# Scheduling priorities by place in an image's course, for a four-stage kernel on pairs of images

## The chip, the cores and the metric

The kernel runs on one core of a Trainium2 chip. The metric is the device time of one execution in microseconds (us). Engines are named PE (TensorE, matrix products), PEld (its weight loads), DVE (VectorE), ACT (ScalarE), POOL (GpSimd) and SP (SyncE, which here only issues transfers). DMA means the core's 16 transfer engines. A line such as L1442 is line 1442 of the kernel before; the change inserts lines, so in the kernel after the same statement stands up to 24 lines lower. This text always uses the numbers of the kernel before, except where it shows a profile of the kernel after.

## What is computed

The input is 16 images of 56x56 positions with 128 channels, in float32. Each image goes through four layers, one after the other. Each adds its result to a running image (the last writes the sum out) after a group norm with 32 groups:

```
x = x + window_attention(gn(x))   # 7x7 windows, shifted by 3; 4 heads; softmax; output product
x = x + triangle(gn(x))           # layer norm, gated products, product over k, layer norm, gate
x = x + fourier(gn(x))            # 2D Fourier modes: attention over the 56 rows as tokens, then two
                                  # operators on modes with a GELU between, instance norms
x = x + bilinear(gn(x))           # products with SiLU, 3x7 convolutions, per-position 16x16 products
```

No layer mixes images, so images are independent. Within an image almost everything depends on what stands before it.

## The kernel before

The kernel is one long program without loops at run time. `tile_blocks` goes over the images b = 0 to 15 and for each writes out load, window attention, triangle, Fourier, bilinear. Images alternate between two **lanes** (`lane[0] = b % 2`). Each lane has its own large work buffer (the arena, one per lane), its own small buffers and its own PSUM banks; the running images `xt` share a pool of two. So two images can be in work at once, and image b+2 can begin only when image b has given up its lane's arena and its `xt`.

The order of the instructions on each engine isn't written by hand. A scheduler takes the program, keeps a model of each engine's time, and whenever an engine is free gives it, of the instructions whose inputs and buffers are ready, the one with the best (lowest) priority number. The priority is a counter of the context, `tc.cur_priority`, that rises as the program is traced. So in the kernel before, every instruction of image b comes ahead of every instruction of image b+1, where both are ready; image b+1 fills what is left. The result is a fixed order for each engine, which then runs it strictly in that order; semaphores make it wait where needed. DMA issues stand in the queue of the engine that issues them: SP the loads, stores and most of bilinear's transfers, ACT bilinear's writes to DRAM, POOL the table's.

The parts of one image that the steps of the prediction name:

- **Load** (L450 to L457): seven transfers, transposes on PE, a copy on ACT. Then the group norm of each layer (L420 to L440), a chain of small steps.
- **Window attention** (L527 to L625): eight rows of windows, each a chain of products, softmax and products.
- **Triangle** (L628 to L735): the two layer norms, the gated products in two parts (L689 to L715), a turn (L724), the gate.
- **Fourier, first part** (L1155 to L1175): column modes (L918), scores (L1104) on DVE, and the modes called x3 (L1174).
- **Fourier, table loop** (L1203 to L1235): 8 steps of 8. Each step fetches 2 x 294 KB of a table from DRAM on POOL's queue (L1209), multiplies on DVE (L1211) and contracts on PE. There are eight slots for what is fetched.
- **Fourier, tail** (L1238 to L1301): a first inverse transform, then two operators (`operator`, L918 to L1032), each a chain of modes, product, inverse and norm; Gelu (L1290) ends the first.
- **Bilinear** (L1330 to L1510): 7 steps, each with project (SiLU, L1354), convolutions, and contractions. A contraction writes one tile eight times over to DRAM (L1342, 1.8 MB, ACT's queue), reads it back spread over partitions (L1439, 448 KB each, SP's queue), multiplies on DVE (L1442) and sums on PE (L369, L372).

The lines around the change are these:

```
    for b in range(NB):
        lane[0] = b % 2
        xt = load_image(b)
        done = False
        for s in stages:
            done = run[s](b, xt)
```

Of the kernel before, what the change touches and what calls it, by code (L numbers as in the profile page):

```python
# [54 lines left out]
ROWC = NW * WIN  # L55
NEG = -1.0e30
SN = math.sqrt(28.0 * 64.0)


def _rho(r, cut):  # L60
# [248 lines left out]
def tile_blocks(ctx: ExitStack, tc: tile.TileContext, ins, out, at, stages=(0, 1, 2, 3)):  # L309
# [17 lines left out]
    ps2 = [pool(f"ps2_{k}", 1, space=PSUM) for k in range(2)]  # L327

    lane = [0]
    count = [0]  # L330

    def uid(s):
# [127 lines left out]
    def store_image(b, xt):  # L460
        for q in range(NCH):
# [8 lines left out]
                in_=t[:TT, :].rearrange("p (a c) -> p a c", a=4),  # L470
            )

    env = dict(locals())
    blocks = [_window_attention, _triangle, _fourier, _bilinear]
    run = {s: blocks[s](env) for s in stages}
    for b in range(NB):
        lane[0] = b % 2
        xt = load_image(b)
        done = False
        for s in stages:  # L480
            done = run[s](b, xt)
        if not done:
            store_image(b, xt)
# [7 lines left out]
def _window_attention(env):  # L491
    e = _Env(env)
# [34 lines left out]
    def run(b, xt):  # L527
# [8 lines left out]
        for k in range(2):  # L536
            nc.gpsimd.memset(ar[:, k * half_arena + ROWC : k * half_arena + 408], 0.0)
        for wi in range(NW):
            o = wi % 2 * half_arena
            xw, qt, vt, st, atn, ot = (  # L540
                ar[:, o + a : o + a + n]
# [84 lines left out]
def _triangle(env):  # L626
    e = _Env(env)
    nc, mm, tt, ts, act, C, W, bc = e.nc, e.mm, e.tt, e.ts, e.act, e.C, e.W, e.bc  # L628
    eps = e.persistent("eps1", [P, 1], 1e-5)
    HC = 32  # L630

    def layer_norm(chunk, dst, sqs, lw, lb):


        for q in range(NCH):
            d, sq = dst[:, q * CH : (q + 1) * CH], sqs[:, q * CH : (q + 1) * CH]
            src = chunk(q)
            p = e.psb()
            mm(p[:, :CH], lhsT=C("cen"), rhs=src, start=True, stop=True)
            act(sq, p[:, :CH], AF.Square)  # L640
            nc.vector.tensor_copy(d, p[:, :CH])

        pv = e.psb()
        e.together(
            dict(
                out=pv[32 * (q % 4) : 32 * (q % 4) + 32, :CH],
                lhsT=C("oh")[:, 1 - q // 4 : 33 - q // 4],
                rhs=sqs[:, q * CH : (q + 1) * CH],
                start=q < 4,
                stop=q > 2,  # L650
            )
            for q in range(NCH)
        )
        rs = e.w2()
        act(rs[:, :CH], pv[:, :CH], AF.Sqrt, bias=eps)
        nc.vector.reciprocal(rs[:, :CH], rs[:, :CH])
        for q in range(NCH):
            d = dst[:, q * CH : (q + 1) * CH]
            p = e.psb()
            row = 32 * (q % 4) + q // 4  # L660
            mm(p[:, :CH], lhsT=C("ident")[:, row : row + 1].to_broadcast([P, P]), rhs=rs[:, :CH], start=True, stop=True)
            tt(d, d, p[:, :CH], ALU.mult)
            act(d, d, AF.Identity, bias=W("ln")[:, lb : lb + 1], scale=W("ln")[:, lw : lw + 1])

    def run(b, xt):
        nm, rs = e.group_norm(xt)
        ar = e.arena()
        xh = ar[:, 0:3144]
        nc.gpsimd.memset(xh[:, NTOK:], 0.0)

        def normed(q):
            t = e.w2()
            ts(t[:, :CH], xt[:, q * CH : (q + 1) * CH], nm, rs, ALU.add, ALU.mult)
            return t[:, :CH]

        sqs = ar[:, 10312 : 10312 + NTOK]
        layer_norm(normed, xh, sqs, 0, 1)

        l3, r3 = (ar[:, o : o + T * HC].rearrange("p (c i) -> p i c", i=T) for o in (3144, 4936))
        o3 = ar[:, 6728 : 6728 + 64 * T].rearrange("p (j c) -> p c j", c=64)
        for part in range(2):
            for g in range(T // 8):
                p = e.psd()
                for i in range(8):
                    c0 = (8 * g + i) * T
                    for half, w in ((0, "w1a"), (64, "w1b")):
                        mm(  # L689
                            p[half : half + 64, i // 4, i % 4 * P : (i % 4 + 1) * P],  # L690
                            lhsT=xh[:, c0 : c0 + 64],
                            rhs=W(w).rearrange("p (k c) -> p k c", c=64)[:, :, HC * part : HC * part + HC],
                            start=True,
                            stop=True,
                        )
                pv = p.rearrange("p a (i c) -> p (a i) c", c=P)
                sg = e.w2()
                s3 = sg.rearrange("p (i c) -> p i c", c=64)
                act(s3, pv[:, :, 64:128], AF.Sigmoid)
                tt(l3[:, 8 * g : 8 * g + 8, :], pv[:, :, 0:32], s3[:, :, 0:32], ALU.mult)  # L700
                nc.vector.scalar_tensor_tensor(  # L701
                    r3[:, 8 * g : 8 * g + 8, :], pv[:, :, 32:64], 1.0 / T, s3[:, :, 32:64], ALU.mult, ALU.mult
                )
            for g in range(4):
                for half in (0, 64):
                    p = e.psb()
                    s = slice(half, half + T)
                    for c in range(8):
                        mm(p[s, c * T : (c + 1) * T], lhsT=l3[s, :, 8 * g + c], rhs=r3[s, :, 8 * g + c], start=True, stop=True)
                    dst = o3[s, 8 * (4 * part + g) : 8 * (4 * part + g + 1), :]  # L710
                    src = p[s, :CH].rearrange("p (c j) -> p c j", j=T)
                    if half:
                        nc.scalar.copy(dst, src)
                    else:
                        nc.vector.tensor_copy(dst, src)  # L715

        on = ar[:, 3144 : 3144 + NTOK]
        on3 = on.rearrange("p (i j) -> p j i", j=T)
        for g in range(T // 8):
            p = e.psb()  # L720
            for j in range(8):
                for half in (0, 64):
                    s = slice(half, half + T)
                    mm(p[half : half + 64, j * T : (j + 1) * T], lhsT=o3[s, :, 8 * g + j], rhs=C("ident")[s, half : half + T], start=True, stop=True)  # L724
            nc.scalar.copy(on3[:, 8 * g : 8 * g + 8, :], p[:, :CH].rearrange("p (j i) -> p j i", i=T))
        layer_norm(lambda q: on[:, q * CH : (q + 1) * CH], on, sqs, 2, 3)
        for q in range(NCH):
            s = slice(q * CH, (q + 1) * CH)
            pg, py = e.psb(), e.psb()
            mm(pg[:, :CH], lhsT=W("gout"), rhs=xh[:, s], start=True, stop=True)  # L730
            mm(py[:, :CH], lhsT=W("pout"), rhs=on[:, s], start=True, stop=True)
            sg = e.w2()
            act(sg[:, :CH], pg[:, :CH], AF.Sigmoid)
            tt(sg[:, :CH], py[:, :CH], sg[:, :CH], ALU.mult)
            tt(xt[:, s], xt[:, s], sg[:, :CH], ALU.add)  # L735

    return run


def _fourier(env):  # L740
    e = _Env(env)
# [145 lines left out]
    def inorm(y, k):  # L887

        _, rs = centered(y)
        ts(rs, rs, sc[:, k : k + 1], None, ALU.mult)  # L890
        scaled(y, y, rs, k)
# [144 lines left out]
    def attention(uv, ar):  # L1036
# [3 lines left out]
        for s in range(2):  # L1040
# [4 lines left out]
            t = e.w2()  # L1045
# [7 lines left out]
        t = e.w2()  # L1053
# [20 lines left out]
        for name in ("dx", "dya", "dyb"):  # L1074
# [6 lines left out]
            else:  # L1081
                t = e.w2()
# [9 lines left out]

        n = 0
        for bank in range(2):
            sp = e.psb()
            for l0 in (0, 4):
                for c in range(2):
# [41 lines left out]
        for g in range(2):  # L1139
            p = e.psb()  # L1140
            for i in range(4):
                q = 4 * g + i
# [7 lines left out]
            ts(by_row(dst)[:, s], by_row(xt)[:, s], nm, rs, ALU.add, ALU.mult)  # L1150

    def run(b, xt):
        nm, rs = e.group_norm(xt)
        ar = e.arena()
        xa = ar[:, 7056:10640]  # L1155
# [10 lines left out]
        at = attention(uv, ar)  # L1166


        x3 = ar[:TT, : 3 * NM].rearrange("p (k n) -> p k n", k=3)
        for g in range(8):  # L1170
            p = e.psb()
# [23 lines left out]
        spec = x3[:, 0, :]  # L1195
        n = 0
        for q in range(8):
            s = slice(q * STEP, (q + 1) * STEP)
            if q % 2:
                pa, pb = e.psb(), e.psb()  # L1200
# [4 lines left out]
            for two in range(8):  # L1205
                t = slots[n % 8]
# [28 lines left out]
            nc.scalar.copy(spec[:, s], p)  # L1235


        y = ar[:, NM : NM + NTOK]  # L1238
        y3 = y.rearrange("p (t j) -> p j t", j=T)
        turned = ar[:, 7168 : 7168 + NTOK]  # L1240
# [30 lines left out]
        def residual(t0, p):  # L1271
            d = y[:, t0 * T : (t0 + 8) * T]
            tt(d, p, d, ALU.add)

        vs = ar[:, 5376 : 5376 + 4 * CH]
        inverse(ar, [spec], residual, vs)
        an = ar[:, 5376:8960]
# [4 lines left out]
        p12 = ar[:, 8960:12544]  # L1282
        f = ar[:, 0:3584]
        vs = ar[:, 3584:5376]
        operator(ar, an, "mw0r", "mw0i", f, p12, f, vs, 3)
        nc.gpsimd.memset(by_row(f, True), 0.0)
        for q in range(NCH):
            an8, f8 = (by_row(t)[:, 8 * q : 8 * q + 8] for t in (an, f))
            stt(f8, an8, sc[:, 12:13], f8, ALU.mult, ALU.add)
            act(f8, f8, AF.Gelu, bias=shift)  # L1290
        m = an
        operator(ar, f, "mw1r", "mw1i", m, p12, m, vs, 4, sc[:, 14:15])
        for q in range(NCH):
            m8, f8 = (by_row(t)[:, 8 * q : 8 * q + 8] for t in (m, f))
            stt(m8, f8, sc[:, 14:15], m8, ALU.mult, ALU.add)
        inorm(m, 5)
        for q in range(NCH):
            x8, m8 = (by_row(t)[:, 8 * q : 8 * q + 8] for t in (xt, m))
# [5 lines left out]
def _bilinear(env):  # L1304
    e = _Env(env)
# [9 lines left out]
    part = 96 * PLANE // P // 3  # L1315
# [7 lines left out]
        return bass.AP(tensor=t.tensor, offset=t.offset + start, ap=[list(d) for d in dims])  # L1323

    def run(b, xt):
        nm, rs = e.group_norm(xt)
        ar = e.arena()
        kv_dram = padded[e.lane[0]]
# [153 lines left out]
        queries, kern, feat = {q: project(q) for q in range(2)}, {}, {}  # L1482
        spread(0, 0)
        for q in range(NCH + 4):
            if 0 <= q - 4:
                last(q - 4, *feat.pop(q - 4))
            if q + 2 < NCH:
# [39 lines left out]
```

## Time and profile before

| what | value |
|---|---|
| median of 3 runs | 12942.06 us (12939.57 to 12974.12) |
| the profiled execution's own time | 12942.02 us |
| its span, first to last instruction | 12940.2 us |
| mean granted PE clock | 0.872 |
| DMA | 2092.81 MB, mean 162 GB/s |
| queues, share of 16 engines' span | SP's 19.1%, POOL's 17.7%, ACT's 13.3% |
| DVE L1442 | 2648.4 us in 1344, 2019 ns each |
| DVE L1211 | 1563.3 us in 1024, 1552 ns each |
| ACT table loads | 119 of 1283 ns |

How to read it: busy time is the union of an engine's instructions, and a share is of the span. The span can be cut into 40 equal slices, where a digit is the busy share in tenths; or into stretches of one's own choice, with the busy time of each engine and the DMA share in each. Idle time of an engine is put down to what came last before it went on, so of a wait for several things only the last is named. Matmul ends are modelled, so a busy PE isn't PE at its peak. A span is 1.9 us shorter than the execution's time, because what lies before the first and after the last instruction isn't in it.

### The profile page before, as it was taken

The page shows a single profiled execution, that of the slowest core. Times are in us where ns is not written, and L with a number is a line of the kernel's source. Part 1 is how long each engine was busy: PE and PEld are TensorE (multiplying, and loading weights), DVE is VectorE, ACT ScalarE, POOL GpSimd, SP SyncE. Part 2 cuts the span into 40 slices and gives each one's busy share as a digit, 9 for nine tenths or more (in the row PEclk, how much of TensorE's full clock was granted, in tenths as well). Part 3 has the DMA queues.
Part 4 walks back from the last instruction along what each step waited for, and adds up shares of the span by engine and source line. Part 5 has one row for each costly group of instructions (what it writes and reads, how often), then busy time and mean ns, then how long its engine had stood idle before and what let it go on. Part 6 is the DMA issues. An engine that isn't in the chain of part 4 may idle for free. (4 is left out here: it accounts for less than half of the span.)

```text
span 12940.2 us, 198571 instructions
## 1 busy us (share of the span) xinstructions
PE 9941.9 (77%) x81312; PEld 5481.7 (42%) x81312; DVE 9365.3 (72%) x12257; ACT 3739.1 (29%) x6439; POOL 2346.8 (18%) x3131
## 2 busy tenths in 40 slices
PE   7787678876888767887788876878768887687876
PEld 4443254442544325443254432544325453254532
DVE  7775777757777577775877757777577775867757
ACT  4322142231422314223142231422314223142321
POOL 0133001330012300123101230012300123001230
PEclk9887888888988889888898888988889888898888
DMA  1255902659026590355903569035690356903469
GB/s 36 58 182 195 341 29 69 171 199 334 32 83 157 198 339 28 87 153 203 342 21 82 158 210 338 18 92 148 212 333 21 96 145 234 324 8 106 134 236 317
DMA packets 1090458, 2092.81 MB, mean 162 GB/s; under 512 B 97936, under 2 KB 973712, under 8 KB 1089296
## 3 DMA queue, kind: packets, MB, share of 16 engines
q1 hardware_dynamic: 560000, 823.91, 19.1%
q0 software_dynamic: 163840, 616.76, 17.7%
q10 hardware_dynamic: 365712, 639.44, 13.3%
q8 instruction: 644, 10.55, 0.3%
q14 instruction: 262, 2.15, 0.1%
HBM read 1412.69 MB, written 667.03 MB: 161 GB/s over the span
## 5 line engine op out<-in xcount | busy, mean ns | idle before, releaser
L1442 DVE TENSOR_TENSOR arena<-arena 128x1792 f32<-128x1792 f32 x1344 | 2648.4, 2019 | 652.5 <-PE psb L372 349.3
L1211 DVE TENSOR_TENSOR arena<-arena 112x1344 f32<-112x1344 f32 x1024 | 1563.3, 1552 | 322.4 <-DMA arena<-table 310.4
L372 PE MATMUL psb<-arena,cst 128*32 128x448 f32 x9792 | 1505.2, 649 | 0.0
L1209 POOL DMA_DIRECT2D arena<-table x2048 | 1050.7, 515 | 2206.3 <-DMA arena<-table 496.5
L369 PE MATMUL psb<-arena,cst 128*32 128x448 f32 x1408 | 792.3, 650 | 813.7 <-DVE arena L1442 760.4
L372 PE MATMUL psb<-arena 128*64 128x448 f32 (+2 forms) x4864 | 1248.5, 534 | 0.0
L369 PE MATMUL psb<-arena 112*64 112x448 f32 (+1 forms) x1280 | 689.0, 624 | 374.2 <-DVE arena L1104 201.9
L417 POOL TENSOR_TENSOR arena<-arena,power 112x32 f32<-112x32 f32 x224 | 828.6, 3718 | 119.8 <-DVE arena L1373 118.4
L372 PE MATMUL psd<-arena 112*64 112x224 f32 (+1 forms) x3072 | 725.6, 457 | 0.0
L372 PEld LDWEIGHTS psb<-arena 112*64 112x64 f32 (+1 forms) x4864 | 455.3, 155 | 526.8 <-issue 521.1
L1427 ACT COPY arena<-psd 128x896 f32<-128x896 f32 x336 | 304.1, 906 | 1236.1 <-DVE arena L1442 656.6
L369 PE MATMUL psd<-arena 112*64 112x448 f32 x1024 | 539.9, 612 | 133.3 <-DVE arena L1211 117.6
L369 PEld LDWEIGHTS psb<-arena,cst 128*32 128x32 f32 x1408 | 120.3, 118 | 1211.5 <-DVE arena L1442 966.4
L1104 DVE TENSOR_TENSOR arena<-w,coef 128x1792 f32<-128x1792 f32 x256 | 508.0, 2018 | 81.4 <-PE psb L372 71.0
L372 PEld LDWEIGHTS psb<-arena,cst 128*32 128x32 f32 x9792 | 360.6, 123 | 448.2 <-issue 427.4
L372 PE MATMUL psd<-arena,wgt 128*32 128x448 f32 x2688 | 502.8, 608 | 38.8 <-DMA arena<-padded 38.3
L689 PE MATMUL psd<-wgt,arena 128*64 128x128 f32 x7168 | 493.3, 283 | 49.3 <-DVE arena L701 38.9
L369 PE MATMUL psd<-arena,wgt 128*32 128x448 f32 x896 | 440.7, 611 | 79.9 <-DMA arena<-padded 42.2
L689 PEld LDWEIGHTS psd<-wgt,arena 128*64 128x64 f32 x7168 | 425.4, 139 | 179.5 <-issue 126.8
L918 PE MATMUL psb<-cst,arena 128*128 128x64 f32 (+1 forms) x2688 | 447.6, 340 | 54.3 <-ACT arena L928 25.6
L918 PEld LDWEIGHTS psb<-cst,arena 128*128 128x128 f32 x2688 | 439.0, 255 | 93.2 <-issue 50.6
L1341 ACT COPY w<-psb 128x448 f32<-128x448 f32 x336 | 178.7, 532 | 1006.5 <-PE psb L372 749.9
(305 smaller groups left out, 18845.8 us busy)
## 6 DMA issues: line engine op xcount, KB each, us to landing
arena<-table POOLq DMA_DIRECT2D x2048, 294.0 KB, 9.1
dy<-w ACTq DMA_DIRECT2D x336, 1792.0 KB
arena<-dy SPq DMA_DIRECT2D x1344, 448.0 KB
arena<-padded SPq DMA_DIRECT2D x896, 162.8 KB
w<-x SPq DMA_DIRECT2D x112, 224.0 KB
out<-w SPq DMA_DIRECT2D x112, 224.0 KB
padded<-w ACTq DMA_DIRECT2D x336, 62.0 KB
padded<-arena SPq DMA_DIRECT2D x6, 449.5 KB
```

What stands on the lines that cost most here:

```text
L369: done = mm(**first)
L372: mm(**kw)
L417: ptt(dst, src, w, ALU.pow)
L689: mm(p[half : half + 64, i // 4, i % 4 * P : (i % 4 + 1) * P], lhsT=xh[:, c0 : c0 + 64], rhs=W(w).rearrange("p (k c) -> p k c", c=64)[:, : ...
L918: mm(p[:, 2 * i * nl : 2 * (i + 1) * nl], lhsT=src[:, t * P : (t + 1) * P], rhs=fc, start=True, stop=True)
L1104: tt(t4, bc(ys[c][:, l0 : l0 + 4, :], 1, 8), bc(coef[:, c, h0 : h0 + 8, l0 : l0 + 4], 3, T), ALU.mult,)
L1209: nc.gpsimd.dma_start(out=t[hh * T : (hh + 1) * T, :], in_=bc(tflat[q, two, hh], 0, T))
L1211: tt(t4, bc(x3[:, :, s], 1, 2), t4, ALU.mult)
L1341: nc.scalar.copy(t[:, :CH], p[:, :CH])
L1427: nc.scalar.copy(z, p[:, :, :CH])
L1442: tt(t4, bc(rep, 2, 2), bc(z, 1, 2), ALU.mult)
```

## The change

Each section of an image's course now sets the priority counter, instead of letting it run on from the start of the program. `at_time(t)` sets it to 100 times a place on a common axis: the origin of the image plus t. Origins of pairs are 1640 apart, and within a pair the odd image's origin is 100 later, a sixteenth. So an instruction of image 9 at place t of its course has the same priority as one of image 8 at place t + 100. The places follow the stages: windows 20 to 195, triangle 225 to 440, Fourier 475 to 1085 (x3 620, table loop 646 to 779, tail 800 to 1085), bilinear 1120 to 1550. The scheduler, its model of the engines and all instructions stay.

```diff
+BEAT, LEAD, COURSE, LAG = 100, 1000, 1640, 100
...
+    origin = [0]
...
+    def at_time(t):
+
+        tc.cur_priority = int(BEAT * (origin[0] + t))
+
     env = dict(locals())
     blocks = [_window_attention, _triangle, _fourier, _bilinear]
     run = {s: blocks[s](env) for s in stages}
     for b in range(NB):
         lane[0] = b % 2
+        origin[0] = LEAD + b // 2 * COURSE + b % 2 * LAG
+        at_time(0)
         xt = load_image(b)
...
         for wi in range(NW):
+            e.at_time(20 + 25 * wi)
...
     def run(b, xt):
+        e.at_time(225)
...
         for part in range(2):
+            e.at_time(300 + 40 * part)
...
+        e.at_time(380)
...
         layer_norm(lambda q: on[:, q * CH : (q + 1) * CH], on, sqs, 2, 3)
+        e.at_time(440)
...
     def run(b, xt):
+        e.at_time(475)
...
         for bank in range(2):
+            e.at_time(540 + 35 * bank)
...
+        e.at_time(620)
         x3 = ar[:TT, : 3 * NM].rearrange("p (k n) -> p k n", k=3)
...
         for q in range(8):
+            e.at_time(646 + 19 * q)
...
+        e.at_time(800)
         y = ar[:, NM : NM + NTOK]
...
+        e.at_time(858)
         vs = ar[:, 5376 : 5376 + 4 * CH]
         inverse(ar, [spec], residual, vs)
...
+        e.at_time(910)
         operator(ar, an, "mw0r", "mw0i", f, p12, f, vs, 3)
...
+        e.at_time(1000)
         operator(ar, f, "mw1r", "mw1i", m, p12, m, vs, 4, sc[:, 14:15])
...
+        e.at_time(1085)
         inorm(m, 5)
...
     def run(b, xt):
+        e.at_time(1120)
...
         for q in range(NCH + 4):
+            e.at_time(1170 + 38 * q)
```

## The prediction

> **What bounds the kernel now.** I read the page first, then the busy time by stretch, then the waits, and last the order of the instructions, which tells the two images of a pair apart.
>
> ```profile
> span 12940.2 us, 198571 instructions
> PE 9941.9 (77%) x81312; PEld 5481.7 (42%) x81312; DVE 9365.3 (72%) x12257; ACT 3739.1 (29%) x6439; POOL 2346.8 (18%) x3131
> ...
> DMA  1255902659026590355903569035690356903469
> GB/s 36 58 182 195 341 29 69 171 199 334 32 83 157 198 339 28 87 153 203 342 21 82 158 210 338 18 92 148 212 333 21 96 145 234 324 8 106 134 236 317
> ```
>
> No engine is full on average. The digits of the DMA row repeat eight times in 40 slices: eight pairs of images of some 1,610 us, each with a half almost free of DMA and a last third at nine tenths. To give each record its image I laid the built order of the kernel before beside its trace, engine by engine; records and instructions agree one for one on the vector, scalar and GpSimd engines. For the pair of images 8 and 9 (times of the trace, us): the table loop (L1209) begins about 7003 in image 8 and about 7200 in image 9, and ends at 7186 and 7369; the bilinear stage begins at 7489 and 7617, and ends at 8045 and 8120. Image 9 runs 75 us behind at both ends and about 180 us behind at the table. Image 10's load starts at 8031, its x3 (L1174) at 8608. These marks cut the busy time:
>
> ```profile
> core 0: us, PE busy (x) PEld busy (x) DVE busy (x) ACT busy (x) POOL busy (x), PEclk, DMA share, GB/s
> 7003.00:7186.00 183.00, 148.73 (x877) 70.27 (x878) 153.74 (x133) 17.08 (x35) 63.37 (x124) 0.87 0.80 205
> 7186.00:7369.00 183.00, 157.08 (x1117) 86.29 (x1113) 143.88 (x166) 41.98 (x75) 68.30 (x129) 0.88 0.76 199
> 7369.00:7489.00 120.00, 87.06 (x906) 64.70 (x906) 89.46 (x207) 64.82 (x110) 6.75 (x10) 0.82 0.00 1
> 7489.00:7617.00 128.00, 96.22 (x656) 51.20 (x656) 77.15 (x144) 49.25 (x89) 39.20 (x24) 0.84 0.49 166
> 7617.00:8045.00 428.00, 298.40 (x2032) 122.57 (x2032) 294.67 (x206) 75.43 (x127) 84.67 (x42) 0.88 0.95 336
> 8045.00:8120.00 75.00, 46.39 (x316) 20.88 (x312) 60.10 (x57) 15.79 (x26) 8.86 (x8) 0.85 0.66 218
> 8120.00:8608.00 488.00, 396.68 (x4274) 257.53 (x4274) 348.30 (x616) 204.61 (x345) 23.26 (x56) 0.93 0.04 11
> ```
>
> The columns are length, busy time of PE, weight loads, DVE, ACT, POOL, then clock, DMA share and rate. From image 10's start to its x3 (last row) PE is busy 81% and DVE 71%: compute bound. Both table loops (rows 1, 2) have DVE at 84% and 79% with DMA near 0.8. Then 120 us with no DMA at all: Fourier tails, chains of small steps. Then bilinear: alone 0.49, both images 0.95. So the stage that matters is bilinear, its limit is the DMA engines, and what it costs depends on when its transfers begin and on what runs beside them. In that stage the waits say how little slack there is elsewhere:
>
> ```profile
> PEld psb L369 <- DVE arena L1442: 105.1, 42, 7.7
> PE psb L369 <- DVE arena L1442: 80.4, 40, 6.9
> ```
>
> (us, times, longest, between 7617 and 8045.) PE follows the products of DVE, which follow the replicated tiles that DMA brings.
>
> **What the skill says here.** The Trainium skill, "DMA: Bandwidth & Descriptors", section "Issuing engines are not separate DMA queues": transfers from SP, ACT and POOL end on the same 16 engines and mix there. The trace agrees: 0.95 in the row at 7617 is fed by SP (q1, 19.1% of the span) and ACT (q10, 13.3%) together. So reordering the issues of two images within bilinear adds no bandwidth; I go by that. "ScalarE: Activation LUTs", section "What ACT_TABLE_LOAD costs", gives 1283 ns for a load plus a drain; the trace has the same 1283 ns for each of 119 loads. I take the trace's number and no drain.
>
> **The change part by part.** No instruction of work is added or removed; the scheduler gets other priorities. I compared the two built orders, each instruction weighted by its mean duration in the trace before, and asked: when image 8 reaches a mark on DVE, how far is image 9 (us of its own 620 us of DVE work)?
>
> - *Load, window attention, triangle, up to x3: nothing.* Image 9 stands at 171 us before and 173 after when image 8 reaches x3. Same cover, same cost.
> - *Table loops.* POOL's issues stay image by image (96 of image 8's in a row before, 92 after; then image 9's). But image 9's multiplies (L1211) now go ahead of image 8's first inverse: image 8 reaches its first operator (L918) when image 9 stands at 322 to 332 instead of 289. From image 8's x3 to the end of image 9's table loop DVE has 307 us instead of 318, at 0.81 busy: that loop ends 13 us earlier.
> - *Tails.* When image 8 enters bilinear, image 9 stands at 388 to 394 (before 375): 14 us more of DVE in a stretch that is 0.85 busy, +16 us. When image 9 enters, image 8 stands at 441 instead of 457: −18 us of DVE at 0.81, −22 us. The time of image 8 alone in bilinear shrinks from 128 to 90 us. What hid image 8's first operator, image 9's table loop, is gone; now its cover is image 9's inverse.
> - *Bilinear.* DMA-time before: 0.49×128 + 0.95×428 + 0.66×75 = 63+407+50 = 520 us. After, the lone stretch carries 0.49×90 = 44, 19 less; at 0.95 that is +20 us. Image 9's end: −22+20 = −2.
> - *End of the pair.* When the next image's SP loads come up, image 9 has 13 to 18 of its 147 SP transfers left instead of 23 to 31, so 31 us of DMA-time instead of 50. Image 8's end: −22+(520−44−31−407)/0.95 = +18. The lag would fall from 75 to 55 us.
> - *What queues behind that.* DVE's order puts the same 15 us of the next image's work (group norm and first window row) among image 9's last products in both kernels. DVE runs in order, so image 9 cannot end before image 10's load, norm and first row have passed. That chain took 89 us in the trace (8031 to 8120) beside full DMA; image 11's norm and first row, undisturbed, took 34 us (8121 to 8155), and the loads were some 30 us: about 62. So the end is at +18+62−75 = +5, not −2. The next front half has as much done as before, so its x3 moves by the same +5.
> - *ACT tables.* Loads fall from 119 to 103 in the order, all of it in Gelu against SiLU (15+15 to 8+8) where image 9's first operator no longer mixes with image 8's bilinear: at most 16×1.283 = 20 us; ACT is at 49 of 128 us there, so I take half, −10.
> - *SP and ACT issues in bilinear* alternate a little more (SP 326 runs of one image for 306, over five images). Bounds: no trace shows its price. Above, DMA share 0.93 for 0.95, which on 445 us is +10 us a pair; below, 0.98 (slices of the trace reach 0.99 to 1.01), −14 us. I take 0.
>
> Sum: 8×5−10 = +30 on the profiled run's 12,942.0 (2 us beside its span; the median of the three runs is 12,942.06): **12,970 us**.
>
> **The rivals.**
>
> *A, the forecast: the shifts cancel.* For it: both orders do the same by x3 and hold the same DVE work at the pair's end. Its own range is 12,880 to 13,060.
>
> *B, slower: image 8's delay is handed on.* Place: the boundary of the pair. If the next image's first chain keeps its 75 us beside full DMA, image 9 ends at +18, and the lane of image 9, too. Price 18×8 = 144, so 13,086; with the DMA share at 0.93, 80 more, 13,166. It decides from the point where the lag at the end stays above 57 us. For it: 0.66 DMA share there and loads that wait for it. Against: much of the 75 us was image 9's own leftover. I put it at 13,100.
>
> *C, faster: bilinear fills better.* If image 8 enters bilinear at +11 rather than +16 (image 9's table loop shares DVE with less), both images meet sooner and DMA runs at 0.98: −22 on the 476 us after image 9's start, ×8 = −176, less 20 of table loads at most: 12,750 at the best. Likely half to all: 12,780. For it: the only stretch with no DMA and no full engine (7369 to 7489) would have two chains in it instead of one and a half.
>
> *D, it does nothing:* 12,942, within A; the orders differ, so only as a sum of zero.
>
> **Numbers.** A 0.42, B 0.33, C 0.25. Within A, 0.08 ends faster by over 0.3% (39 us, about what a measurement of this kernel can tell from no change), 0.20 within, 0.14 slower. Faster 0.33, same 0.20, slower 0.47. The range goes from C's best with some 40 us for the table loops' earlier end (12,710) to B with the poorer share and 60 us for stalls that in-order queues may meet when the tails overlap (13,230).
>
> **What would show it.** Right: image 8 enters bilinear some 16 us later after its x3 and image 9 some 22 us earlier; lone stretch near 90 us; DMA share of the joint stretch 0.95; lag at the end 55 to 65 us; 103 table loads; front half unchanged. Wrong: a lag that stays at 75 with a longer period (B), a share near 0.98 (C), or a joint stretch in which DVE waits for DMA or PE much longer than 62 us before L1442. If the front half itself moves by over 10 us a pair, the forecast fails at its first step.

## The result, and the profile after

The changed kernel took 13,092.1 us (median of 4 runs, 13,079.1 to 13,139.8) beside 12,958.1 us for the kernel before in the same comparison (4 runs): 1.0106 times as long, 95% interval 1.0069 to 1.0143. It is slower. The time lies within the stated range, but it is near that of rival B (13,100), not of the forecast (12,970). The profiled execution took 13,079.1 us with a span of 13,077.4; before it was 12,942.0 and 12,940.2. The difference to explain is 137 us, 17 us for each of eight pairs.

The page of the kernel after, the same lines as were shown of before:

```profile
span 13077.4 us, 198471 instructions
...
PE 10072.0 (77%) x81312; PEld 5509.6 (42%) x81312; DVE 9341.9 (71%) x12257; ACT 3727.3 (29%) x6423; POOL 2333.1 (18%) x3131
...
DMA  1255902569035690256903569035690356903568
GB/s 36 57 181 194 336 29 72 166 214 326 19 81 157 211 326 23 81 157 214 335 10 85 153 234 318 8 94 144 243 314 3 99 139 229 323 8 101 137 242 306
```

DVE and POOL have slightly less busy time, ACT has 16 instructions fewer (the table loads, 119 before and 103 after). The rhythm of eight is the same, but the last slice of a pair carries 306 to 336 GB/s where it carried 317 to 342. As in the forecast, each record is given its image by laying the built order beside the trace. For the pair of images 8 and 9 the marks of after are: x3 of image 8 at 7073, the last of the small products behind its table loop (L1254) at 7271, the end of image 9's loop at 7413, bilinear entered at 7560 (image 8) and 7639 (image 9), left at 8119 and 8184, x3 of image 10 at 8687. The busy time between them, with the columns of before (length, PE, weight loads, DVE, ACT, POOL, clock, DMA share, rate):

```profile
core 0: us, PE busy (x) PEld busy (x) DVE busy (x) ACT busy (x) POOL busy (x), PEclk, DMA share, GB/s
7073.00:7271.00 198.00, 165.79 (x1026) 82.26 (x1027) 173.02 (x150) 23.47 (x48) 72.54 (x143) 0.89 0.77 212
7271.00:7413.00 142.00, 123.35 (x773) 66.35 (x770) 115.14 (x134) 34.21 (x58) 55.72 (x110) 0.92 0.74 224
7413.00:7560.00 147.00, 119.58 (x1167) 85.49 (x1168) 107.67 (x245) 78.18 (x137) 8.84 (x15) 0.78 0.00 1
7560.00:7639.00 79.00, 56.98 (x439) 29.70 (x438) 48.54 (x104) 27.77 (x52) 28.59 (x16) 0.79 0.44 150
7639.00:8119.00 480.00, 339.36 (x2204) 141.46 (x2204) 317.74 (x223) 84.63 (x141) 92.05 (x44) 0.83 0.93 326
8119.00:8184.00 65.00, 43.07 (x281) 17.18 (x273) 51.42 (x54) 14.27 (x25) 7.73 (x11) 0.79 0.62 202
8184.00:8687.00 503.00, 414.95 (x4292) 263.79 (x4293) 349.51 (x620) 203.89 (x346) 22.90 (x56) 0.90 0.04 10
```

Row by row against before (183, 183, 120, 128, 428, 75, 488 us): the stretch from image 8's x3 to the products behind its table loop is longer, image 9's loop ends sooner after it, the stretch with no DMA is 27 us longer, the lone stretch 49 us shorter, the joint stretch 52 us longer at a DMA share of 0.93 for 0.95. The marks of before in this comparison are up to 7 us off those of after (image 8's bilinear ended at 8045 there; by its last product on DVE, as here, at 8038); the means below use one rule for both.

One pair wanders by some 10 us, so the readings below are means over the pairs that begin with images 2 to 12. Times are us after the even image's x3 (the first instruction of that section on DVE or ACT); the lag is the odd image's end less the even one's, the period runs to the next even image's x3.

| | before | after | difference |
|---|---|---|---|
| odd image's table loop ends | 366.4 | 350.7 | −15.7 |
| even image enters bilinear | 485.5 | 501.6 | +16.1 |
| odd image enters bilinear | 614.0 | 575.1 | −38.9 |
| even image ends | 1,037.1 | 1,065.7 | +28.6 |
| odd image ends | 1,115.9 | 1,120.2 | +4.3 |
| next even image's x3 (period) | 1,610.7 | 1,626.4 | +15.7 |
| joint stretch, DMA share | 423.1, 0.946 | 490.7, 0.924 | +67.6 |

The seven periods from image 0's x3 to image 14's are longer by 111 us together; the course of the last pair from there adds 20, the time up to the first x3 adds 6: 137.

**Where the even image is held up.** Its Fourier tail begins with some small steps on DVE. In before, the first of them copies two columns out of a result of PE (L1245), and DVE does it as soon as PE has them (start, length, instruction, in brackets the idle time ahead of it and what ended that):

```profile
7189.33 0.16 DVE L1245 COPY lessmean<-psb 112x2 f32<-112x2 f32 x1 [0.72 <-PE psb L1244]
```

In the kernel after, the same steps of image 8 on PE, DVE and ACT:

```profile
7253.81 0.35 PE L1262 MATMUL psb<-lessmean,cst 56*112 56x2 f32 x2
...
7255.06 10.37 DVE L1228 TENSOR_TENSOR arena<-arena 112x1344 f32<-112x1344 f32 x7 [1.34 <-DMA arena<-table]
7265.35 0.15 DVE L1263 COPY lessmean<-psb 112x2 f32<-112x2 f32 x1
...
7265.61 0.69 ACT L1283 ACTIVATE w<-psb,lessmean 112x512 f32<-112x512 f32 x1 [9.78 <-DVE lessmean L1263]
```

L1228 is the table multiply, here of image 9. PE's result lay ready at 7254.2; DVE first waited 1.3 us for a row of image 9's table and then did seven of its products, so that the copy came 11 us late, and ACT waited 9.8 us for it. In the means this copy stands 178.6 us after x3 in before and 196.3 in after (+18), while the table loop itself (its last copy, L1235) ends at 180.0 and 186.4 (+6). A product that waits for a transfer holds up whatever stands behind it on its engine. The Trainium skill ("TensorE: Matmul & The Clock Gate", section "Architectural detail: the array is 16× 32×32, not 1× 128×128") calls ACT's and DVE's queues strictly first in, first out; these records agree.

The first inverse follows, which DVE brings out of PE's results by two copies (L960, L973 in the kernel after). In the kernel before:

```profile
7193.28 0.62 DVE L960 COPY arena<-psd 128x448 f32<-128x448 f32 x1 [0.44 <-PE psd L956]
7201.30 0.62 DVE L960 COPY arena<-psd 96x448 f32<-96x448 f32 x1 [7.40 <-PE psd L956]
```

and in the kernel after:

```profile
7268.60 0.61 DVE L973 COPY arena<-psd 128x448 f32<-128x448 f32 x1
7269.13 1.55 DVE L1228 TENSOR_TENSOR arena<-arena 112x1344 f32<-112x1344 f32 x1
...
7309.18 0.41 PE L969 MATMUL psd<-cst,arena 112*32 112x112 f32 x2
...
7311.08 1.56 DVE L1228 TENSOR_TENSOR arena<-arena 112x1344 f32<-112x1344 f32 x1 [1.07 <-DMA arena<-table]
7312.56 0.61 DVE L973 COPY arena<-psd 96x448 f32<-96x448 f32 x1
```

The two copies stood 8 us apart, now they stand 44 us apart (means of the six pairs: 7.8 and 45.8). Here DVE's own order counts for little: PE ended the last product for the second copy (L969) at 7309.6, 3 us before the copy. On PE these products of image 8 stand among the contractions of image 9's table products, and those follow DVE one product at a time, most of them after a wait of about a microsecond for the next table row.

### The profile page after: what moved, and what is told of

Its sections match the earlier page's. It is cut to its first block, busy times and chain, and to the rows that moved or that the text cites. A ratio compares the mean times of both kernels' runs of the same rounds, so it can differ in the third digit from the quotient of the medians.

```text
span 13077.4 us, 198471 instructions
## 1 busy us (share of the span) xinstructions
PE 10072.0 (77%) x81312; PEld 5509.6 (42%) x81312; DVE 9341.9 (71%) x12257; ACT 3727.3 (29%) x6423; POOL 2333.1 (18%) x3131
## 5 line engine op out<-in xcount | busy, mean ns | idle before, releaser
L1228 DVE TENSOR_TENSOR arena<-arena 112x1344 f32<-112x1344 f32 x1024 | 1569.8, 1552 | 363.2 <-DMA arena<-table 350.1
L419 POOL TENSOR_TENSOR arena<-arena,power 112x32 f32<-112x32 f32 (+1 forms) x224 | 841.2, 3775 | 115.3 <-DVE arena L1396 109.0
L374 PE MATMUL psd<-arena,wgt 128*32 128x448 f32 x2688 | 532.8, 636 | 27.3 <-DMA arena<-padded 27.1
L700 PE MATMUL psd<-wgt,arena 128*64 128x128 f32 x7168 | 501.7, 284 | 67.6 <-DVE arena L712 42.7
L371 PE MATMUL psd<-arena,wgt 128*32 128x448 f32 x896 | 460.0, 634 | 105.0 <-ACT arena L1450 56.5
```

The source lines that it names most:

```text
L371: done = mm(**first)
L374: mm(**kw)
L419: ptt(dst, src, w, ALU.pow)
L700: mm(p[half : half + 64, i // 4, i % 4 * P : (i % 4 + 1) * P], lhsT=xh[:, c0 : c0 + 64], rhs=W(w).rearrange("p (k c) -> p k c", c=64)[:, : ...
L1228: tt(t4, bc(x3[:, :, s], 1, 2), t4, ALU.mult)
```

## The theories

**T**: an image's own chain sets the time of its lane. The change lets the odd image's table products and their contractions go ahead of the even image's first steps of the tail on DVE and PE, so the even image enters bilinear 16 us later. The odd image enters 39 us earlier and takes its share of the DMA engines, so the even image ends 29 us later, and the next image of its lane can start only then (same arena and image tile). The odd image's gain is lost in the stretch that DMA limits: its bilinear stage takes 545 us for 502.

**S**, the main rival: the even sharing of DMA between the two images in bilinear costs the time by itself, whatever happens in the tails. Others: the marks in themselves, the front half, or the sum of work (DMA-time or DVE-time) setting the period whoever is first.

One of these fell without a run. With COURSE 3280 and LAG 1640, so that images follow one another as in the program, the kernel with all the marks builds into exactly the order of the kernel before on all five engines. The marks alone do nothing; only the relation between the two images does.

## The experiments

The first five undo the change for a part of the even image's course, by this edit of the kernel after with another interval each time:

```
-        tc.cur_priority = int(BEAT * (origin[0] + t))
+        ahead = 400 if lane[0] == 0 and 620 <= t < 1120 else 0
+        tc.cur_priority = int(BEAT * (origin[0] + t - ahead))
```

**1. Even image first in table loop and tail** (620 to 1120, as shown).

> Even images get 400 us of head start in priority from x3 to the end of the Fourier tail (places 620 to 1120); elsewhere the priorities of the kernel after. The built order of this kernel is that of the kernel before up to the bilinear stage (image 9 stands at 375 us of its DVE work when image 8 enters bilinear, 457 the other way) and that of the kernel after's rule in bilinear. Theory T (the loss is made in the tail, where image 8's first operator is put behind image 9's table products, and is then handed on because the next image of that lane starts when image 8 ends): ratio to before 0.999 to 1.004, image 8's x3 to bilinear back from 501 to 486 us, period of the even lane 1606 to 1612. Theory S (the loss is made in bilinear, where DMA is shared evenly between the images so that image 8 ends late): ratio 1.006 to 1.010, bilinear of even images at least 13 us longer than before.

Measured: 0.9998 [0.9978, 1.0017]. The whole loss is gone, with the rule of the change still in force in bilinear and in the front half. By the time between marks of this kernel:

```profile
core 0: us, PE busy (x) PEld busy (x) DVE busy (x) ACT busy (x) POOL busy (x), PEclk, DMA share, GB/s
...
7370.00:7491.00 121.00, 88.19 (x893) 65.14 (x892) 87.89 (x201) 64.28 (x108) 6.57 (x10) 0.81 0.00 1
7491.00:7617.00 126.00, 95.47 (x652) 50.93 (x653) 77.39 (x144) 48.83 (x88) 39.18 (x24) 0.84 0.51 173
7617.00:8057.00 440.00, 315.02 (x2081) 129.30 (x2079) 303.98 (x212) 76.87 (x128) 81.40 (x39) 0.85 0.94 334
```

The stretch without DMA (121) and the lone stretch (126) are those of before, and the two copies are 8 us apart again. The joint stretch is still 15 us longer and the even image ends 10 us later (means), yet the period is 1,610.5 for 1,610.7. S's own sign is nearly there, since the even image's bilinear is 12.4 us longer; but the next front half is 10.1 us shorter, and nothing of it reaches the total (the table at the end of the experiments).

**2. Even image first in bilinear only** (from 1120 on).

> Even images get 400 us of head start in priority in bilinear only (places from 1120 on); elsewhere the priorities of the kernel after. The built order in table loop and tail is that of the kernel after (image 9 at 393 us when image 8 enters bilinear). Theory T: still slow, ratio 1.006 to 1.012, image 8's x3 to bilinear 500 us or more. Theory S: most of the loss gone, ratio 1.000 to 1.005, bilinear of even images back from 564 to about 552 us.

Measured: 1.0058 [1.0038, 1.0077], between the ranges of T (from 1.006) and S (to 1.005). The even image still enters bilinear at 502. About half of the loss stays although DMA is no longer shared evenly (the odd image's bilinear stage takes 528 us, 545 in after, 502 before). So S is not the cause by itself: experiment 1 removes the loss with the rule of bilinear kept, this one keeps half of it with that rule taken away. (Its traced execution took 13,052 us, median 13,034; there the period is 1,625.1, near that of after.) Sharing adds to a tail that is late already; the two are not additive.

**3. Both** (from 620 on).

> Even images get the head start from x3 to the end of bilinear (places from 620 on); the front half keeps the priorities of the kernel after. Both theories: ratio 0.997 to 1.003, lag at the end of the pair 75 us or more. If it is still over 1.005, the loss comes from the front half (load to x3), and both theories fall.

Measured: 0.9982 [0.9966, 0.9998], period 1,601.4. The front half alone in the new order costs nothing.

**4. The table loop only** (620 to 800), and **5. the tail only** (800 to 1120).

> The head start of even images (400 us of priority) in the table loop only (places 620 to 799); the rest has the priorities of the kernel after. In the built order image 8's first inverse is back at 222 us of image 9's DVE work (before 222, after 238) and its first operator at 292 (289, 322). Theory T with the delay made in the table loop: x3 to the end of the table loop back from 201 to about 181 us, and with it the period of the even lane to 1606 to 1614, ratio 0.999 to 1.004. If the delay is made by image 9's products against image 8's inverse instead, ratio 1.005 to 1.010.

> The head start of even images in the tail only (places 800 to 1119); the rest has the priorities of the kernel after. In the built order the first operator stays at 321 us of image 9's DVE work, as in the kernel after: only the entry into bilinear comes back, from 388 to 381. Theory T with the delay made in the table loop: still slow, x3 to the end of the table loop some 200 us, ratio 1.005 to 1.011. If the tail's own priorities make it, ratio 0.999 to 1.004.

Measured: 1.0020 [1.0007, 1.0034] and 1.0041 [1.0027, 1.0055]. The even image enters bilinear at 483.3 and 488.7, the time up to the small products behind its table loop is 180.9 and 191.4 us (180.5 before, 201.4 after), and the two copies stand some 18 and 16 us apart. These marks are of one execution each, and that of experiment 5 was the shortest of 22 (12,921 us, median 12,996), so they look better than the ratio. Each recovers more than half of the loss: to keep the even image ahead in one of the two parts is nearly enough. Neither is the sole place, and experiment 5 lies between the two readings that I had named for it.

**6. and 7. Is a delay of one image handed on?** To the kernel before, five dependent power operations on POOL ahead of bilinear, in the even images or in the odd ones (`b % 2 == 1`):

```
+        if b % 2 == 0:
+            d, held = e.sm(), e.sm()
+            e.ptt(d[:, 0:32], bc(rs[:, 0], 1, 32), e.power[:, :32], ALU.pow)
+            for k in range(4):
+                o, i = (32, 0) if k % 2 == 0 else (0, 32)
+                e.ptt(d[:, o : o + 32], d[:, i : i + 32], e.power[:, :32], ALU.pow)
+            nc.vector.scalar_tensor_tensor(held[:, 0:1], d[:, 0:1], 0.0, rs, ALU.mult, ALU.add)
+            rs = held[:, 0:1]
```

> The kernel before, with a chain of five dependent operations on POOL (3.7 us each, some 19 us with the steps between) put into even images alone, between the group norm and the bilinear stage; the engines' work is the same but for POOL, idle there. Theory T (an image's own path sets its lane's period, and a delay of the even image is handed on to the next): period longer by 12 to 20 us, ratio 1.007 to 1.012. Rival (the period is set by shared work or by DMA, which goes on meanwhile): ratio 0.999 to 1.004.

> The same chain in odd images alone. The built order then lets the odd lane fall further behind (image 9 starts when image 8 has 58 us of DVE work done, before 15). Theory T says that either lane hands on its delay, but the odd image comes second in priority and was waiting for shared engines and DMA in much of its course, so less of it should count: ratio 1.002 to 1.010. If it counts like the even image's, 1.007 to 1.012; if only the even lane matters, 0.999 to 1.002.

The length of the delay is read from the groups of POOL with shapes kept apart (busy us, mean ns, idle before). Even images delayed:

```profile
L1332 POOL TENSOR_TENSOR sm<-sm,power 128x32 f32<-128x32 f32 x32 | 175.4, 5482 | 2.5
...
L1329 POOL TENSOR_TENSOR sm<-sm,power 128x32 f32<-128x32 f32 x8 | 43.6, 5448 | 0.7
```

odd images delayed:

```profile
L1332 POOL TENSOR_TENSOR sm<-sm,power 128x32 f32<-128x32 f32 x32 | 192.9, 6027 | 2.2
...
L1329 POOL TENSOR_TENSOR sm<-sm,power 128x32 f32<-128x32 f32 x8 | 49.3, 6164 | 0.6
```

So the even images were held up by (175.4+43.6)/8 = 27.4 us each, 219 in all, and the kernel took 1.0152 times as long [1.0126, 1.0177], +197 us: nine tenths of the delay came out at the end, while nearly all of the core's other work was unchanged. That is above T's range because the delay is longer than the 19 us I had reckoned with. T holds; the sum of work does not set the period. The odd lane, which was not delayed itself, was held up too: image 15 ended at 13,140 us (12,937 before). The odd images' delay was 30.3 us each, 242 in all, and cost 1.0174 [1.0145, 1.0202], +225 us. I had expected less from the odd lane; that was wrong. The trace shows how: the lanes come apart. Image 14 of the even lane ends at 12,822 us (12,862 before), image 15 of the odd lane at 13,176 (12,937 before). The even lane did not follow the odd one, and the slower lane sets the total. So the next even image doesn't wait for the odd image's end: its x3 came 392 us after it, for 495 before.

**8. No lag and 9. a lag of 250 between the images of a pair** (kernel after with one constant changed, `LAG` 100 to 0 or 250).

> LAG 0 for 100: no distance in priority between the images of a pair. In the built order both reach x3 and bilinear almost together (image 9 stands at 219 us of its DVE work when image 8 reaches x3, at 428 when image 8 enters bilinear; before 171 and 375). Theory T (what delays the even image's own path is handed on, and what the odd image gains is lost in the shared bilinear stage): clearly slower than the kernel after, ratio 1.015 to 1.05, x3 to bilinear of image 8 well over 500 us. Rival (only the detail of the order at 100 is bad, not the even treatment): ratio 0.995 to 1.01.

> LAG 250 for 100. The distance is then larger than what the lanes reach by themselves (75 to 187 us in the trace before), so the even image comes first nearly everywhere, and the built order is close to that of the kernel before (image 9 at 163, 286 and 380 us of its DVE work when image 8 reaches x3, its first operator and bilinear; before 171, 289, 375). Theory T: ratio 0.996 to 1.003. Rival (priorities by place do harm by themselves): 1.005 to 1.011.

Measured: 1.0531 [1.0508, 1.0554] at 0, just above T's range, 0.9982 [0.9971, 0.9993] at 250; with 1.0106 at 100 the loss shrinks steadily as the even image's lead in priority grows. At 0 the images 8 and 9 do everything together:

```profile
core 0: us, PE busy (x) PEld busy (x) DVE busy (x) ACT busy (x) POOL busy (x), PEclk, DMA share, GB/s
7394.00:7722.00 328.00, 243.32 (x1305) 110.83 (x1304) 222.50 (x188) 20.73 (x50) 131.53 (x244) 0.81 0.86 221
7722.00:7953.00 231.00, 156.97 (x1685) 117.47 (x1684) 163.48 (x381) 122.86 (x210) 13.12 (x19) 0.79 0.00 1
7953.00:8505.00 552.00, 397.79 (x2549) 165.24 (x2553) 364.49 (x264) 98.68 (x167) 122.75 (x59) 0.85 0.91 325
```

Both table loops, then both tails with no DMA for 231 us (120 in before), then both bilinear stages at 0.91. The stages that DMA feeds no longer cover the tails of the other image. That is the far end of what the change begins. At 250 the lone stretch is 129 us and the lag at the end 79, as before.

**10. Half a period between the images of a pair.** The kernel before, with image 1's first load held until image 0's table loop has ended; after that nothing forces the distance:

```
+    gate = persistent("gate", [P, 1])
...
+            if b == 1 and q == 0:
+                nc.vector.tensor_copy(t[:TT, 0:1], gate[:TT])
...
+        if b == 0:
+            nc.vector.tensor_copy(e.gate[:TT], spec[:, NM - 1 : NM])
```

> The kernel before (priorities by the order of the program) with one wait more: image 1's load starts only when image 0's table loop is done, through a one-column copy of a kept tile that image 0 writes then. In the built order the lanes then stay half an image apart (image 9's group norm when image 8 has 322 of 620 us of DVE work done, image 8's entry into bilinear when image 9 has 66). If what an image's bilinear costs is set by DMA that both images of a pair want at once, one image's bilinear beside the other's front half, which moves nearly nothing, should cut the period of a pair well under 1606 us (1400 to 1500), and the whole to 0.92 to 0.98 of before, with some 500 us of one lane idle at each end. If the lanes' own chains set the period (each lane's image takes its 1600 us whatever runs beside it), the period stays near 1606 and the whole is 1.03 to 1.05 of before.

Measured: 1.0705 [1.0655, 1.0755], outside both ranges. The page of this kernel:

```profile
span 13867.0 us, 198854 instructions
...
PE 10405.9 (75%) x81312; PEld 5698.6 (41%) x81312; DVE 9360.8 (68%) x12259; ACT 3918.4 (28%) x6570; POOL 2332.3 (17%) x3132
...
DMA  0425447253563526546273652826438263473437
```

DMA is spread: six of the 40 slices reach 7 or 8 and none 9, where before every pair had one at 9. Even so the period is some 1,675 us, and image 0, alone for most of its course, takes 1,316 us. An even image's bilinear is shorter (429 us for 551), but an odd one's is longer (564 for 502), and the way from the even image's end to the next x3 is longer (794 for 574), above all in window attention: some 330 us beside the other's bilinear, for some 190 before. So to keep the two bilinear stages apart does not shorten the period in this arrangement; the run does not tell why window attention is so much longer there.

**11. The kernel after once more** (a blank line added), beside other runs of before.

> The kernel after once more, beside the other distances on the same chip. Every theory: ratio 1.006 to 1.013, image 8's x3 to bilinear 500 us or so.

Measured: 1.0138 [1.0112, 1.0163], a little above the range. Its marks are those of after within 3 us (even image enters bilinear at 499.8 and ends at 1,066.8, period 1,628.7).

**The period of the even lane in three parts**, means of the six pairs in us, from one traced execution each (that of experiment 3 was 39 us shorter than its median). The last column is the part of the third up to the first window row's addition to the next image (L621).

| | x3 to bilinear | bilinear | its end to next x3 | period | up to first row |
|---|---|---|---|---|---|
| before | 485.5 | 551.5 | 573.6 | 1,610.7 | 82.3 |
| after | 501.6 | 564.2 | 560.7 | 1,626.4 | 67.1 |
| experiment 1 | 483.0 | 563.9 | 563.5 | 1,610.5 | 70.2 |
| experiment 2 | 502.1 | 560.9 | 562.1 | 1,625.1 | 70.1 |
| experiment 3 | 479.7 | 549.2 | 572.5 | 1,601.4 | 82.0 |

In after, and likewise in experiment 1, the longer bilinear of the even image and the shorter way to the next x3 nearly cancel (+12.7 and −12.9; +12.4 and −10.1). What is left is the tail: +16.1 in after, −2.5 in experiment 1. The shortening is complete by the first window row, in a stretch that runs beside the odd image's last bilinear products, which end 79 us after the even image in before and 55 and 64 us in after and experiment 1.

## Why the prediction was right or wrong

- **"Load, window attention, triangle, up to x3: nothing."** From its load to its x3 the next even image takes 558.5 us for 571.5. By the prediction's own sign (a front half that moves by over 10 us a pair) this step failed, though no cost arises here. The gain lies in the load, norm and first window row, which the prediction treats under "What queues behind that", below.
- **Table loops, "that loop ends 13 us earlier".** 15.7. Right.
- **Tails, "+16 us" for image 8.** +16.1. Right, and the cause is the one named, image 9's multiplies ahead of the first inverse. The way there is not a simple shift: the first operator begins 41 us later (281 for 240 us after x3) and the second only 15 us later (402 for 387).
- **Tails, "−22 us" for image 9.** −38.9; the lone stretch is 73.5 us and not 90. Mis-sized: I took it from how far image 8's DVE work stands when image 9 enters. Image 9's own tail took 224 us from the end of its table loop for 248, on top of a loop that ended 15.7 us sooner.
- **Image 8's end, "+18".** +28.6. **This is the step that failed.** The cause was right, the size was not. Its sum is image 9's entry (−22), then 38 us more DMA-time in the joint stretch at a share of 0.95 (+40), and nothing for a lower share ("I take 0"). Measured are −38.9, then 53 us more DMA-time (490.7×0.924 = 453 for 423.1×0.946 = 400; +56 at 0.946), and +11 for the share of 0.924 in place of 0.946, in sum the +28.6 within rounding. The +11 is the worse of the two bounds that the prediction gives for it (0.93, +10 us). The waits of that stretch show how it comes. In after, between 7639 and 8119 (us, times, longest):

```profile
PEld psb L371 <- DVE arena L1465: 116.8, 43, 12.4
PE psb L371 <- DVE arena L1465: 95.9, 37, 11.6
```

The longest wait of PE for DVE's products is 12 us, for 7 to 8 before. What these products wait for in their turn is in DVE's group of the same stretch (busy, mean ns, then idle before and its releasers), of before between 7617 and 8045

```profile
L1442 DVE TENSOR_TENSOR arena<-arena 128x1792 f32<-128x1792 f32 x136 | 267.6, 2019 | 61.8 <-PE psb L372 29.2 <-DMA arena<-dy 21.2 <-ACT arena L1427 5.8
```

and of after:

```profile
L1465 DVE TENSOR_TENSOR arena<-arena 128x1792 f32<-128x1792 f32 x147 | 289.2, 2018 | 71.7 <-DMA arena<-dy 36.8 <-PE psb L374 27.9 <-ACT arena L1450 6.8
```

The idle time put down to DMA rose from 21 to 37 us, that put down to PE did not.

- **"What queues behind that": 62 for 75, so image 9's end "+5, not −2", and x3 "by the same +5".** The first chain did shorten: −15.2 us up to the first window row and −12.9 up to x3, for the forecast's −13. But x3 moved by +15.7, since it follows image 8's end: 28.6−12.9 = 15.7, where the forecast had 18−13 = +5. Nearly all of the 10.7 us that x3 missed is thus the 10.6 of image 8's end, 85 us in eight pairs. The next load's first copy on ACT begins 2.1 us after image 8's last product on DVE in before and 2.2 in after, which shows the tie; experiments 6 and 7 show it too. The offsets of the means alone would not: from the even image's end to the next x3 it is 556 to 577 us, from the odd image's 488 to 577, over all kernels but those of experiments 7 and 10.
- **Image 9's end, "+5".** +4.3, with a lag of 54.5 us for the forecast 55. Luck in part: the lag is 43 to 46 us in three of the six pairs and 63 to 65 in the others. In the latter some 14 us of the next image's DVE work stand ahead of image 9's end, as in before; in the former 8.5 us, and not "the same 15 us".
- **Rival B** said what happened in its name ("image 8's delay is handed on"), and its time was near. That is partly luck: it took the 18 us that was really 28.6, and a first chain that "keeps its 75 us" where the way to x3 became 12.9 us shorter, and the two misses nearly cancel. Its stated deciding point, a lag that stays above 57 us, was wrong: the lag fell to 54.5 and the delay was handed on all the same.
- **Table loads, 103.** 103, of which the part in Gelu and SiLU fell by 14 and not by all 16 (the other two are in triangle, L699). Of the 10 us taken off for them no gain is to be seen; their 16×1.283 = 20.5 us at most are not separated from the rest by any run. The Trainium skill's figure ("ScalarE: Activation LUTs", "What ACT_TABLE_LOAD costs") for the load itself is that of the trace.

Open is how much of the loss is the granted clock of PE, told of below, and why the joint stretch reaches a lower DMA share in after. Even sharing alone does not lower it: experiment 1 has the same rule in bilinear and reaches 0.948 in the mean.

Two kernels ended below before by a little, with intervals just under 1: the even image first from its table loop on (0.9982) and a lag of 250 (0.9982). They have the lead of before in table loop and tail; 0.2%, barely clear of noise, is all that these priorities brought.

## What to carry to other kernels

When two streams take turns on in-order engines, fairness between them can have a price, as here: the stream that is behind puts instructions that still wait for a transfer ahead of the leader's ready ones, and each such wait is the leader's. Ask for each lane what its next item of work waits for, and tie a shift to that lane's own end, not to the end of the pair. Here a lead of some 180 us at the table loops let one image's transfers cover the other's small steps, and bringing the images into step cost 5%. That is no rule for any distance: half a period between the images, which puts the stage full of transfers beside the one full of products, cost 7%.

## What the hardware showed that I had not expected

- A power operation of POOL on 128x32 elements took 5.4 to 6.2 us in the added chains. I had sized the delay by the mean of 3.7 us of a group that mixes 112x32 (5.6 us) with 112x8 (1.9 us): a group's mean over several forms is no duration.
- The granted clock of PE fell as the kernels became slower: 0.872 before, 0.863 after, 0.838 both with no lag and with half a period between the images, although the matrix products are the same 81,312. PE's busy time was 9,942 us before and 10,072, 10,024 and 10,406 us in these three. In the stretch without DMA ahead of bilinear it was 0.81 before and 0.78 after (means). Whether the lower clock makes part of the loss or only follows from the gaps was not separated by any run. In experiment 1 PE's busy time was 10,016 us at a clock of 0.868, more than half of the rise, in a kernel that lost nothing.
- With half a period between the images no slice of the page shows the DMA engines at nine tenths, and the kernel was slower by 7%.
